# Involution tap matrices: pixel-innermost in whole tiles instead of in groups of three pixels

## The chip, the cores and the metric

One core of one Trainium2 chip runs the whole program. The metric is device time in microseconds (us), the median of 3 runs: 1796.4 us before the change (1794.46 to 1797.01). All data are float32.

## The reference, cut to what matters

Four residual layers act on x of shape (4, 256, 56, 56), each on a group-normed input. Layers 0 and 2 are involutions: from the normed input a 1x1 convolution gives 64 channels, a second one gives, for each of 16 groups and each pixel, 49 tap weights, and each output pixel is the weighted sum of its own 7x7 window. Layer 1 is two 3x3 convolutions, layer 3 a gating; the change does not touch them.

```python
h = jnp.einsum('bchw,oc->bohw', x, reduce_w) + reduce_b[None, :, None, None]
kern = jnp.einsum('bchw,oc->bohw', h, span_w) + span_b[None, :, None, None]
kern = kern.reshape(b, G, 1, K * K, Ho, Wo)            # G = 16, K = 7
out = (kern * patches).sum(axis=3)                     # patches: the 7x7 windows
```

## The kernel before, in words

An image is cut into 19 x 7 = 133 tiles of 3 x 8 = 24 pixels (`NT`, `TP`). The windows of the 24 pixels of a tile lie in one field of 9 x 14 = 126 input positions (`Q`). So the involution of a tile and a group is a matrix product: the 126 positions x 16 channels of the input against a matrix of 126 positions x 24 pixels, in which each pixel has its 49 weights at its own window and zeros elsewhere. These are the tap matrices, the tile `kt`.

Work goes by units: an image b (4) and a half of the channels cb (2), so 8 units in layer 0 and 8 in layer 2. A unit has two stages, one after the other on TensorE.

The first stage, `tap_matrices`, makes `kt` for 8 groups, 24 pixels and 133 tiles, in 32 steps n. A step handles two groups and three pixels (`PB` = 3): TensorE multiplies a weight field by the hidden channels `hp` (line 593, moving operand 133 tiles in one run), six products into one of four pairs of PSUM banks. Then an eviction adds the bias and copies to `kt`. Of three steps in a row, the first two are evicted by VectorE, one instruction for 2 x 3 x 133 = 798 elements a partition (line 611), and the third by ScalarE, six instructions of 133 elements (line 604). So a unit has 22 evictions by VectorE and 10 by ScalarE. `hooks` puts small steps of other work (group-norm sums, loads, channel means) between the steps n. `kt` has one buffer: the next unit's first eviction comes after this unit's last product.

The second stage, `apply`, goes over 7 columns of tiles, tx. For each column and each tile row it multiplies the windows `xw` (stationary) by a slice of `kt` (moving, line 635): 10 tile rows with 4 groups at once (96 moving columns, two products side by side in the array, over 64 output channels each), then 9 tile rows with 2 groups at once (48 moving columns, four side by side). ScalarE takes the first group of the result out of PSUM (line 648 in layer 0, 650 in layer 2), VectorE adds the other groups (655), and GpSimd (660, layer 0) or VectorE (662, layer 2) adds it to the image. After the products of a column, TensorE transposes the strip of a column three ahead (line 406), ScalarE copies it out (418), DMAs on the SP queue and, in layer 0, one on GpSimd's make shifted copies (424, 426), and GpSimd (391, layer 0) or ScalarE (389, layer 2) writes the next strip into the only strip buffer. The next column's transposes wait for that.

The order on each engine is the order in which the program writes the instructions: `in_order` ties each instruction to the one before it on its engine. Nothing is reordered when one takes longer.

In the layout before, `kt` is [126, 8 groups, 8 triples of pixels, 133 tiles, 3 pixels]. An eviction by VectorE writes, for each of two groups, 399 elements in one run. One by ScalarE writes every third element, 12 bytes apart. A slice for line 635 is a group's 24 pixels of one tile: 8 runs of 12 bytes, 1596 bytes apart.

Of the kernel before, what the change touches and what calls it, by code (L numbers as in the profile page):

```python
# [10 lines left out]
F32 = mybir.dt.float32  # L11
# [13 lines left out]
GB = P // GC  # L25
# [10 lines left out]
Q = QY * QX  # L36
NTY, NTX = -(-H // TY), W // TX
NT = NTY * NTX
TP = TY * TX
# [4 lines left out]
PB = 3  # L44
# [27 lines left out]
def net_kernel(  # L72
# [226 lines left out]
    def involution_layer(layer, xin, xout, red, span, sb, xs_of, ahead=None, pending=None):  # L299

        with ExitStack() as es:
            wpool = es.enter_context(tc.tile_pool(name="iw", bufs=1))
            big = es.enter_context(tc.tile_pool(name="ibig", bufs=1))
# [3 lines left out]
            def two_banks():  # L307

                return banks.tile([P, 2, 512], F32, name="ps")
# [83 lines left out]
            def window(ty):  # L393

                k, j = divmod(ty, TY)
                return (0, NSB, 2 * NSB - 1)[j] + k
# [185 lines left out]
            def tap_matrices(b, cb, hooks):  # L582

                hp = h_of[b]
                kt = big.tile([Q, GB, TP // PB, NT, PB], F32, name="kt")
                for n in range(GB // 2 * TP // PB):
                    gp, pb = divmod(n, TP // PB)
                    ps = two_banks()
                    for k in range(PB):
                        py, px = divmod(pb * PB + k, TX)  # L590
                        z0 = ZF - py * QX - px
                        for i in range(2):
                            nc.tensor.matmul(  # L593
                                ps[:Q, i, k * NT : (k + 1) * NT],
                                z_sb[i * R : (i + 1) * R, cb * GB // 2 + gp, z0 : z0 + Q],
                                hp[i * R : (i + 1) * R, py, px].rearrange("p a t -> p (a t)"),
                                start=True,
                                stop=True,
                            )
                    g0, p0 = 2 * gp, pb * PB  # L600
                    if n % 3 == 2:
                        for i in range(2):
                            for k in range(PB):
                                nc.scalar.activation(  # L604
                                    kt[:, g0 + i, pb, :, k],
                                    ps[:Q, i, k * NT : (k + 1) * NT],
                                    AF.Identity,
                                    bias=zb_sb[:, cb * GB + g0 + i, p0 + k : p0 + k + 1],
                                )
                    else:  # L610
                        nc.vector.tensor_tensor(  # L611
                            kt[:, g0 : g0 + 2, pb],
                            ps[:Q, :, : PB * NT].rearrange("q i (k t) -> q i t k", k=PB),
                            zb_sb[:, cb * GB + g0 : cb * GB + g0 + 2, p0 : p0 + PB]
                            .unsqueeze(2)
                            .to_broadcast([Q, 2, NT, PB]),
                            ALU.add,
                        )
                    for h in hooks.get(n, ()):
                        h()  # L620
                return kt

            def apply(b, cb, kt, tx, xw):

                img = xs_of[b, cb].rearrange("p (h w) -> p h w", w=W)
                y0 = 0
                for ng, tys, nty, rows in O_PARTS:
                    pair = two_banks()
                    nb, m = len(tys), ng * GC
                    v = pair[:, :nb, : ng * nty * TP].rearrange("p i (e n) -> p i e n", e=ng)  # L630
                    for i in range(nb):
                        for k in range(nty):
                            ty = tys[i] + k
                            for j in range(P // m):
                                nc.tensor.matmul(  # L635
                                    v[m * j : m * j + m, i, :, k * TP : (k + 1) * TP],
                                    xw[:, window(ty), m * j : m * j + m],
                                    kt[:, ng * j : ng * j + ng, :, ty * NTX + tx, :],
                                    start=True,
                                    stop=True,  # L640
                                )
                    n = rows // nb * TX
                    o = [v[:, :, e, :n] for e in range(ng)]
                    un = work.tile([P, 2, O_PARTS[0][3] // 2 * TX], F32, name="un")
                    un = un.rearrange("p i n -> p (i n)")[:, : rows * TX]
                    part = un.rearrange("p (i n) -> p i n", i=nb)
                    if layer == 0:
                        nc.scalar.mul(part, o[0], bn["par"][ng][:, 0:1])  # L648
                    else:
                        nc.scalar.activation(  # L650
                            part, o[0], AF.Identity, bias=bn["t4"][:, cb : cb + 1], scale=bn["s4"][ng][:, 0, cb : cb + 1]
                        )
                    for e in range(1, ng):
                        s = bn["par"][ng][:, e : e + 1] if layer == 0 else bn["s4"][ng][:, e, cb : cb + 1]
                        nc.vector.scalar_tensor_tensor(part, o[e], s, part, ALU.mult, ALU.add)  # L655
                    dst = img[:, y0 : y0 + rows, tx * TX : (tx + 1) * TX]
                    y0 += rows
                    u = un.rearrange("p (r x) -> p r x", x=TX)
                    if layer == 0:
                        nc.gpsimd.tensor_tensor(dst, u, dst, ALU.add)  # L660
                    else:
                        nc.vector.scalar_tensor_tensor(dst, u, 0.0, dst, ALU.max, ALU.add)
# [355 lines left out]
            for u, (b, cb) in enumerate(units):  # L1018
                hooks = hooks0 if u == 0 else {}
                if prev is not None:  # L1020
                    pb, pc, st, last_sums = prev
# [31 lines left out]
                elif last_image:  # L1053
                    place(hooks, g2, (1,))
                    hooks.setdefault(16, []).append(ahead[0])
                kt = tap_matrices(b, cb, hooks)

                begin_windows()
# [48 lines left out]
                for tx in range(NTX):  # L1107
                    if layer == 2 and u == len(units) - 1 and tx == NTX - 1:
                        column_sums(tx - 1)
                    for f in early[tx]:  # L1110
                        f()
                    apply(b, cb, kt, tx, xws[u * NTX + tx])
                    next_windows()
                    next_strip()
                    if tx > 0 and not (layer == 2 and u == len(units) - 1 and tx == NTX - 1):
                        column_sums(tx - 1)
                    for f in late[tx]:
                        f()
# [640 lines left out]
```

## Time and profile before

| | us |
|---|---|
| median of 3 runs | 1796.4 |
| span of the profiled execution | 1791.4 |
| PE busy in it | 1716.7 (96%) |
| VectorE (DVE) busy | 1385.3 (77%) |
| ScalarE (ACT) busy | 813.5 (45%) |
| GpSimd (POOL) busy | 406.2 (23%) |

The profiled execution's own time is its span from the first to the last instruction; what lies around the span makes up the 5.0 us by which the median of the runs is longer. In the trace each float32 product of the program is two weight loads and two matmuls (PEld and PE), so line 593 has 6144 matmuls for 3072 products. A line of the groups names the source line, the engine, the operation, what is written and read, the shapes, and the count; then busy time, mean duration of one in ns, and the idle time of the engine before it with what ended it. Durations of neighbours on an engine overlap, so the distance from start to start is shorter than the duration. A line of the timeline has the start in us, the time from the first start to the last end, and the same names; x112 at its end means that 112 instructions are merged in it.

### The profile page before, as it was taken

The page shows a single profiled execution, that of the slowest core. Times are in us where ns is not written, and L with a number is a line of the kernel's source. Part 1 is how long each engine was busy: PE and PEld are TensorE (multiplying, and loading weights), DVE is VectorE, ACT ScalarE, POOL GpSimd, SP SyncE. Part 2 cuts the span into 40 slices and gives each one's busy share as a digit, 9 for nine tenths or more (in the row PEclk, how much of TensorE's full clock was granted, in tenths as well). Part 3 has the DMA queues.
Part 4 walks back from the last instruction along what each step waited for, and adds up shares of the span by engine and source line. Part 5 has one row for each costly group of instructions (what it writes and reads, how often), then busy time and mean ns, then how long its engine had stood idle before and what let it go on. Part 6 is the DMA issues. An engine that isn't in the chain of part 4 may idle for free.

```text
span 1791.4 us, 55774 instructions
## 1 busy us (share of the span) xinstructions
PE 1716.7 (96%) x24040; PEld 1507.5 (84%) x24040; DVE 1385.3 (77%) x2745; ACT 813.5 (45%) x1882; POOL 406.2 (23%) x627
## 2 busy tenths in 40 slices
PE   6999999999999999999999999999999999999998
PEld 4998988889978988898889888986888887788886
DVE  2777787767778988988898889885777778687775
ACT  2555556555533222222323132111767667567564
POOL 2224422444320000000000000001000355463572
PEclk9999999999989999999999999999999999999997
DMA  2445444633653021211111111122344567566653
GB/s 86 135 151 170 140 146 134 196 107 119 204 171 105 32 75 51 76 33 64 58 68 44 52 63 37 44 110 73 122 164 156 162 213 220 169 223 189 183 154 115
DMA packets 66003, 215.76 MB, mean 120 GB/s; under 512 B 13237, under 2 KB 20926, under 8 KB 62046
## 3 DMA queue, kind: packets, MB, share of 16 engines
q1 hardware_dynamic: 49262, 145.37, 25.9%
q0 software_dynamic: 14656, 64.77, 11.3%
q8 instruction: 190, 3.11, 0.7%
q10 hardware_dynamic: 1840, 2.05, 0.4%
q14 instruction: 55, 0.45, 0.1%
HBM read 76.30 MB, written 49.15 MB: 70 GB/s over the span
## 4 chain that ended last, share of the span: by engine, by line
PE 68%; DVE 19%; ACT 4%; DMA 4%; issue 3%; POOL 2%; SPq 1%; POOLq 0%; ACTq 0%; DVEq 0%
PE mm L1523 17%; PE ps L593 14%; PE ps L635 14%; PE mm L1441 9%; DVE kt L611 6%; PE mm L1412 5%; PE ps L406 3%; DMA xw<-xw 3%; DVE un L655 3%; PE ps L469 1%; DVE res L1516 1%; DVE xs L1375 1%; DVE st L1105 1%; ACT kt L604 1%; ACT hp L488 1%
## 5 line engine op out<-in xcount | busy, mean ns | idle before, releaser
L635 PE MATMUL ps<-kt,xw 126*32 126x48 f32 (+1 forms) x12544 | 381.8, 235 | 27.8 <-issue 12.2
L635 PEld LDWEIGHTS ps<-kt,xw 126*32 126x32 f32 (+1 forms) x12544 | 341.9, 121 | 74.5 <-issue 45.5
L593 PE MATMUL ps<-hp,z_sb 64*126 64x133 f32 x6144 | 383.2, 279 | 8.4 <-DVE kt L611 4.6
L1523 PE MATMUL mm<-v,u_sb 128*128 128x280 f32 (+1 forms) x1728 | 383.5, 383 | 1.9 <-DVE u_sb L1254 1.5
L593 PEld LDWEIGHTS ps<-hp,z_sb 64*126 64x126 f32 x6144 | 363.6, 185 | 24.4 <-DVE kt L611 6.8
L611 DVE TENSOR_TENSOR kt<-ps,zb_sb 126x798 f32<-126x798 f32 x352 | 332.9, 980 | 60.4 <-PE ps L593 49.2
L1523 PEld LDWEIGHTS mm<-v,u_sb 128*128 128x128 f32 x1728 | 326.1, 189 | 56.3 <-DVE u_sb L1254 1.9
L604 ACT ACTIVATE kt<-ps,zb_sb 126x133 f32<-126x133 f32 x960 | 280.1, 441 | 107.3 <-PE ps L593 107.3
L1441 PE MATMUL mm<-v,u_sb 128*128 128x252 f32 (+1 forms) x936 | 209.5, 384 | 0.0
L1441 PEld LDWEIGHTS mm<-v,u_sb 128*128 128x128 f32 x936 | 176.4, 189 | 30.5 <-issue 0.8
L655 DVE SCALAR_TENSOR_TENSOR un<-ps,s,un 128x240 f32<-128x240 f32 x224 | 102.6, 458 | 86.7 <-ACT un L650 79.9
L1560 POOL DMA_DIRECT2D x<-xs x24 | 13.1, 547 | 680.1 <-DVE xs L1559 426.5
L655 DVE SCALAR_TENSOR_TENSOR un<-ps,par_sb,un 128x240 f32<-128x240 f32 x224 | 98.1, 457 | 86.8 <-ACT un L648 82.3
L1508 ACT ACTIVATE res<-xs,shift,norm_sb 128x1120 f32<-128x1120 f32 (+1 forms) x24 | 30.2, 1258 | 236.3 <-DVE xs L1559 107.3
L418 ACT COPY xw<-ps 126x896 f32<-126x896 f32 x112 | 101.2, 905 | 44.0 <-PE ps L406 38.5
L406 PE MATMUL ps<-ident_sb,strip_sb 128*126 128x128 f32 x784 | 111.9, 283 | 8.4 <-POOL strip_sb L391 5.3
L660 POOL TENSOR_TENSOR xs<-un,xs 128x240 f32<-128x240 f32 x112 | 72.1, 664 | 192.2 <-DVE un L655 192.1
L648 ACT ACTIVATE un<-ps,par_sb 128x240 f32<-128x240 f32 x112 | 50.1, 448 | 122.5 <-PE ps L635 120.6
L650 ACT ACTIVATE un<-ps,bn_t,s 128x240 f32<-128x240 f32 x112 | 60.1, 537 | 94.7 <-PE ps L635 88.7
L406 PEld LDWEIGHTS ps<-ident_sb,strip_sb 128*126 128x126 f32 x784 | 85.1, 142 | 19.5 <-POOL strip_sb L391 8.3
L1412 PE MATMUL mm<-xs,u_sb 128*128 128x126 f32 (+1 forms) x792 | 98.7, 277 | 2.3 <-DVE xs L1375 1.3
L1412 PEld LDWEIGHTS mm<-xs,u_sb 128*128 128x128 f32 x792 | 94.4, 191 | 3.7 <-DVE xs L1428 1.6
(256 smaller groups left out, 1903.1 us busy)
## 6 DMA issues: line engine op xcount, KB each, us to landing
xw<-xw SPq DMA_DIRECT2D x168, 252.0 KB
xw<-xw SPq DMA_DIRECT2D x224, 126.0 KB
xw<-xw POOLq DMA_DIRECT2D x56, 252.0 KB, 4.6
xs<-x SPq DMA_DIRECT2D x24, 560.0 KB
x<-xs POOLq DMA_DIRECT2D x8, 1568.0 KB, 7.5
xs<-x SPq DMA_DIRECT2D x8, 1568.0 KB
xs<-in_x_dram SPq DMA_DIRECT2D x6, 1568.0 KB
x<-xs SPq DMA_DIRECT2D x6, 1568.0 KB
```

Source lines behind the costliest of these rows:

```text
L406: nc.tensor.transpose(ps[:Q, k * P : (k + 1) * P], flat[:, k * Q : (k + 1) * Q], ident_sb)
L418: nc.scalar.copy(xw[:, :NSB, :], ps[:Q, : NSB * P].rearrange("q (n c) -> q n c", n=NSB))
L593: nc.tensor.matmul(ps[:Q, i, k * NT : (k + 1) * NT], z_sb[i * R : (i + 1) * R, cb * GB // 2 + gp, z0 : z0 + Q], hp[i * R : (i + 1) * R, py ...
L604: nc.scalar.activation(kt[:, g0 + i, pb, :, k], ps[:Q, i, k * NT : (k + 1) * NT], AF.Identity, bias=zb_sb[:, cb * GB + g0 + i, p0 + k : p0 ...
L611: nc.vector.tensor_tensor(kt[:, g0 : g0 + 2, pb], ps[:Q, :, : PB * NT].rearrange("q i (k t) -> q i t k", k=PB), zb_sb[:, cb * GB + g0 : cb ...
L635: nc.tensor.matmul(v[m * j : m * j + m, i, :, k * TP : (k + 1) * TP], xw[:, window(ty), m * j : m * j + m], kt[:, ng * j : ng * j + ng, :, ...
L650: nc.scalar.activation(part, o[0], AF.Identity, bias=bn["t4"][:, cb : cb + 1], scale=bn["s4"][ng][:, 0, cb : cb + 1])
L655: nc.vector.scalar_tensor_tensor(part, o[e], s, part, ALU.mult, ALU.add)
L660: nc.gpsimd.tensor_tensor(dst, u, dst, ALU.add)
L1412: nc.tensor.matmul(ps[:, co * m : (co + 1) * m], u[ci][:, co * P : (co + 1) * P], v2[:, e, : n // 2, ci * WT : (ci + 1) * WT], start=(ci = ...
L1441: nc.tensor.matmul(ps, u1_sb[:, ci, dy, k, co * P : (co + 1) * P], v[:, k, dy * NB + ci : (dy + n - 1) * NB + ci + 1 : NB, :], start=(j == 0),
L1523: nc.tensor.matmul(ps, u2_sb[:, ci, dy, k, co * P : (co + 1) * P], v[:, k, dy * NB + ci : (dy + n - 1) * NB + ci + 1 : NB, :], start=(j == 0),
```

## The change

`kt` becomes [126, 8 groups, 133 tiles, 24 pixels]. A slice for line 635 is now one run of 24 elements, 96 bytes, for each group. An eviction by VectorE writes 266 runs of 3 elements (12 bytes), 96 bytes apart. One by ScalarE writes 133 single elements, 96 bytes apart. The numbers of instructions, elements, PSUM buffers and bytes of `kt` are the same, and so is the order of the instructions on every engine.

```diff
-                kt = big.tile([Q, GB, TP // PB, NT, PB], F32, name="kt")
+                kt = big.tile([Q, GB, NT, TP], F32, name="kt")
...
                                 nc.scalar.activation(
-                                    kt[:, g0 + i, pb, :, k],
+                                    kt[:, g0 + i, :, p0 + k],
                                     ps[:Q, i, k * NT : (k + 1) * NT],
...
                         nc.vector.tensor_tensor(
-                            kt[:, g0 : g0 + 2, pb],
+                            kt[:, g0 : g0 + 2, :, p0 : p0 + PB],
                             ps[:Q, :, : PB * NT].rearrange("q i (k t) -> q i t k", k=PB),
...
                                     xw[:, window(ty), m * j : m * j + m],
-                                    kt[:, ng * j : ng * j + ng, :, ty * NTX + tx, :],
+                                    kt[:, ng * j : ng * j + ng, ty * NTX + tx, :],
```

## The prediction

> **What bounds the kernel now.** I read the shares of busy time first, then the costliest groups, then the timeline of one first stage and one steady column. Page and groups:
>
> ```profile
> PE 1716.7 (96%) x24040; PEld 1507.5 (84%) x24040; DVE 1385.3 (77%) x2745; ACT 813.5 (45%) x1882; POOL 406.2 (23%) x627
> ...
> L635 PE MATMUL ps<-kt,xw 126*32 126x48 f32 (+1 forms) x12544 | 381.8, 235 | 27.8 <-issue 12.2
> ...
> L611 DVE TENSOR_TENSOR kt<-ps,zb_sb 126x798 f32<-126x798 f32 x352 | 332.9, 980 | 60.4 <-PE ps L593 49.2
> ...
> L604 ACT ACTIVATE kt<-ps,zb_sb 126x133 f32<-126x133 f32 x960 | 280.1, 441 | 107.3 <-PE ps L593 107.3
> ```
>
> PE is the engine that is never idle. Both evictions wait for PE (49.2 and 107.3 us), and PE hardly waits for them (in the row of L593, 383.2 us busy, 4.6 us for L611). But how much slack they have is a matter of the first stage alone. Its timeline (start, length, count):
>
> ```profile
> 299.77 8.29 PE L593 MATMUL ps<-hp,z_sb 64*126 64x133 f32 x140
> ...
> 300.44 1.75 ACT L604 ACTIVATE kt<-ps,zb_sb 126x133 f32<-126x133 f32 x6 [0.36 <-PE ps L593]
> 301.13 1.89 DVE L611 TENSOR_TENSOR kt<-ps,zb_sb 126x798 f32<-126x798 f32 x2 [0.17 <-PE ps L593]
> 302.50 1.75 ACT L604 ACTIVATE kt<-ps,zb_sb 126x133 f32<-126x133 f32 x6 [0.31 <-PE ps L593]
> ```
>
> Three steps take 2.06 us (300.44 to 302.50): PE needs three times 0.69, ScalarE 1.75 of it, VectorE 1.89. The slack of each is 0.2 to 0.3 us. A steady column of the second stage in layer 0:
>
> ```profile
> 201.53 0.99 PEld L635 LDWEIGHTS ps<-kt,xw 126*32 126x32 f32 x72 [0.16 <-issue]
> 201.70 0.47 ACT L648 ACTIVATE un<-ps,par_sb 128x240 f32<-128x240 f32 x1 [1.27 <-PE ps L635]
> ...
> 202.60 0.98 PE L406 MATMUL ps<-ident_sb,strip_sb 128*126 128x128 f32 x7
> ...
> 203.51 3.27 PE L635 MATMUL ps<-kt,xw 126*64 126x96 f32 x112
> ...
> 205.58 0.90 POOL L391 TENSOR_SCALAR strip_sb<-xs,norm_sb 128x616 f32<-128x616 f32 x1
> ...
> 206.71 0.55 PE L406 MATMUL ps<-ident_sb,strip_sb 128*126 128x128 f32 x3
> ```
>
> The column is 4.11 us (202.60 to 206.71), PE running through; but the strip (L391) is ready at 206.48, only 0.2 us before the transposes (L406) that need it.
>
> [...] The trace before has a row for ScalarE at exactly the new step, the bias table (written 24 words apart), and one for VectorE writing runs of three (14 words apart):
>
> ```profile
> L281 ACT COPY zb_sb<-ps x1: 1103/1103/1103, 44.3 to 44.3; 126x384 f32<-126x384 f32 x1
> ```
>
> ```profile
> L383 DVE MEMSET strip_sb<- x16: 198/198/198, 34.3 to 1683.8; 128x168 f32 x16
> ```
>
> Copies of 252 and 896 contiguous elements take 366 ns (L1424) and 905 ns (L418): 0.84 ns an element and 155 ns fixed. So L281 pays (1103 - 155) / 384 = 2.47 ns an element[...]. L383 writes 56 runs of three in at most 198 ns, 3.5 ns a run with everything in it; L611 takes 831/266 = 3.1 ns for a run at 1.04 ns an element. So a run of three shows no large price at a step of 14 words. No row shows it at 24.
>
> **Part 1, ScalarE's evictions: longer, and on the path.** Today 441 ns. Contiguous, the same form with a bias would take 259 + 133 x 0.84 = 371 (fixed part from L726: 448 elements in 634 ns), so the 12-byte step costs (441 - 259) / 133 = 1.37 ns an element now. At 2.47: 259 + 133 x 2.47 = 587, that is +146 ns. Six of them, 1.75 us today, take 1.75 + 6 x 0.146 = 2.63. In all 960 x 0.146 = +140 us of ScalarE, of which the slack takes a part. Where it ends: there are four PSUM pairs, so the products of step n+6, two steps after the next ScalarE step, wait for the group of step n+2. Two groups then take 2.63 + 0.17 (release) + 3 x 0.69 + 0.30 (PE to ScalarE) = 5.17 us, 2.58 a group instead of 2.06: +0.52. (ScalarE alone, back to back at 0.26 + 0.146 each, would give 2.44.) A stage has 10 groups, 9 intervals; some are already 2.8 us because norm steps stall PE (405.56, 407.62, 410.47, 412.52, 415.32 in one stage), and these I leave. 6 x 0.52 = 3.1, and 0.35 at the end, where steps 30 and 31 wait for ScalarE's last group but one: 3.45 a unit. 16 units: **+55 us**. Queued behind the late evictions on ScalarE are only hooks and the next column's L648 or L650; PE waits for them through PSUM, and that is counted.
>
> **Part 2, VectorE's evictions.** [...] I take 0.10, because L383 speaks for the low side. Cover: VectorE is busy 22.7 us of a 24.8 us stage (403 to 428 us); 22 x 0.10 makes 24.9 in a stage that part 1 has stretched to 28. Only the end and the norm steps behind it feel it: 0.2 a unit, **+3 us**. Without part 1 as cover it would be up to 2.2 x 16 = 35.
>
> **Part 3, the products read 24 in one run: a gain.** Today 40 loads with 96-column products take 1.99 us in the trace (the row of 40 at 199.37, just before those shown): less one load's 0.14, 1.85/19 = 97 ns a pair; the 72 with 48 columns 0.88/17 = 52 ns a set of four. Contiguous operands cost 0.85 ns a column: L1523 383.5 us for 1152 x 280 + 576 x 224 columns; and L718, four side by side over 448 columns, 14 in 1.70 us, about 382 ns a set, the same. So packing in the array costs nothing, and 97 against 82 and 52 against 41 are the runs of three: 0.47 and 0.69 ns a run. With 4 and 2 runs left: 84 and 42.4. Gain per column: 20 x 13 + 18 x 9.6 = 0.43 us of PE; x 112 = 48 us if PE sets every column. It does not:
> - Layer 0: next late is the strip. From L648 (201.70) to the next possible transposes (206.48 + 0.17) are 4.95 us; then 0.91 to the products, and 2.06 (203.51 to 205.83 is 2.32, less 0.26) to the next L648: 7.92 us for two columns, 3.96 against 4.11. So five steady columns gain 0.15, the first two 0.3 together, the last 0.43: 1.5 a unit, 12 in layer 0.
> - Layer 2: the strip is ScalarE's, ready about 1.2 us early, so PE's columns gain all. But PE waits 45.5 us in 152 gaps for no visible cause ("issue") before L635 loads, most of it in some 20 of its 56 columns; there I count 0.1. 36 x 0.43 + 2 = 17.5.
>
> Together **-30 us**.
>
> **Sum.** +55 + 3 - 30 = +28 us on the span of 1791.4. The median of the runs stands 5.0 above that span; the same on top gives 1796.4 + 28 = 1824. Nothing else moves: the order on each engine and all counts are equal.
>
> **Rivals.**
> - VectorE takes ScalarE's place (0.20). [...] For it: [...]L281. Against: L383[...].
> - The read gain wins (0.12), **faster**. PE gains 0.43 in all 112 columns (-48) while the stages lengthen by only 2.2 us each, because ScalarE runs at 2.44 and norm stalls absorb the rest (+35): 1783. It decides if a stage grows by less than 3.0 us. For it: layer 2 and the stalled intervals. Against: L391's 0.2 us of slack.
> - The reading gains nothing (0.12): the 97 ns are not the runs but something in loading 64 or 32 columns. Then +58: 1854. Against: L718's sets of four with 32-column loads.
> - My case, 0.51, own range 1805 to 1845. Other mishaps, slower: 0.05.
>
> **How the numbers follow.** The likeliest is 1824. The range runs from the low edge of my case beyond it to VectorE's rival, 1798 to 1880, leaving out most of the faster case (0.11) and about 0.07 above. A measurement here can tell about 0.2% (3.6 us) from no change. Faster 0.11 (0.10 of its rival, 0.01 of mine), within 0.2% 0.07 (0.05 mine, the rest the rival's), slower 0.82.
>
> **What would show it.** L604 at about 587 ns, with groups of six starting 2.4 to 2.6 us apart in an undisturbed stretch; L611 under 1.1 us; 96-column loads of 40 in about 1.7 us, 72 in about 0.83; first stages 3 to 4 us longer; steady columns of layer 0 near 3.95, of layer 2 near 3.7, with L406 waiting for L391 longer than before (PE 5.3 us). I am wrong if L604 stays under 500 ns, if L611 passes 1.2 us, or if the 40 loads still take 1.9.

## The result, and the profile after

The changed kernel takes 1812.0 us (median of 4 runs, 1804.5 to 1813.5) against 1796.7 us for the kernel before beside it: ratio 1.0077, 95% interval 1.0057 to 1.0097. The profiled execution has a span of 1811.7 us against 1791.4.

The same rows as before the change, from the page of the changed kernel, and the row of the products of the first stage:

```profile
PE 1682.9 (93%) x24040; PEld 1464.2 (81%) x24040; DVE 1410.5 (78%) x2745; ACT 875.2 (48%) x1882; POOL 407.2 (22%) x627
...
L593 PE MATMUL ps<-hp,z_sb 64*126 64x133 f32 x6144 | 397.6, 280 | 24.0 <-ACT kt L604 16.2
L611 DVE TENSOR_TENSOR kt<-ps,zb_sb 126x798 f32<-126x798 f32 x352 | 353.5, 1042 | 75.7 <-PE ps L593 62.9
...
L604 ACT ACTIVATE kt<-ps,zb_sb 126x133 f32<-126x133 f32 x960 | 344.5, 609 | 82.2 <-PE ps L593 82.2
L635 PE MATMUL ps<-kt,xw 126*32 126x48 f32 (+1 forms) x12544 | 331.5, 224 | 49.3 <-issue 27.2
```

PE's busy time fell by 34 us: L635 lost 50.3 (381.8 to 331.5), so the products do read faster, and L593 grew by 14.4 (383.2 to 397.6). But the span grew by 20, so PE was idle about 54 us longer. Its idle time has a new owner in L593, ScalarE's eviction L604 (16.2 us; before, the largest was L611 with 4.6), and a grown one in L635, the gaps without a visible cause ("issue", 27.2 against 12.2).

I cut the span into the 16 first stages (from the first L593 to the first L635) and the 16 second stages (from there to the next first L593; the last of layer 0 has the convolutions of layer 1 in it):

| us | before | after | difference |
|---|---|---|---|
| first stages | 437.7 | 474.0 | +36.3 |
| second stages | 1276.4 | 1258.6 | -17.9 |
| ahead of the first, behind the last | 77.3 | 79.1 | +1.8 |

So both halves of the change are there, with opposite signs, and the loss is twice the gain. How far such sums can be trusted, one execution each: the eight first stages of layer 2 differ by up to 2.5 us between kernels whose evictions are the same, those of layer 0, where nothing else is changed, by 0.4 or less. I therefore read small differences from the stages of layer 0.

The end of a first stage of layer 0, where no norm step comes between, before (ScalarE alone) and after:

```profile
421.56 1.75 ACT L604 ACTIVATE kt<-ps,zb_sb 126x133 f32<-126x133 f32 x6 [0.30 <-PE ps L593]
423.68 1.75 ACT L604 ACTIVATE kt<-ps,zb_sb 126x133 f32<-126x133 f32 x6 [0.36 <-PE ps L593]
425.73 1.75 ACT L604 ACTIVATE kt<-ps,zb_sb 126x133 f32<-126x133 f32 x6 [0.30 <-PE ps L593]
```

```profile
427.10 4.38 PE L593 MATMUL ps<-hp,z_sb 64*126 64x133 f32 x72 [0.28 <-ACT kt L604]
428.10 4.18 DVE L611 TENSOR_TENSOR kt<-ps,zb_sb 126x798 f32<-126x798 f32 x4 [0.71 <-PE ps L593]
429.47 4.29 ACT L604 ACTIVATE kt<-ps,zb_sb 126x133 f32<-126x133 f32 x12 [0.36 <-PE ps L593]
...
431.75 4.38 PE L593 MATMUL ps<-hp,z_sb 64*126 64x133 f32 x72 [0.27 <-ACT kt L604]
...
434.12 4.28 ACT L604 ACTIVATE kt<-ps,zb_sb 126x133 f32<-126x133 f32 x12 [0.36 <-PE ps L593]
```

ScalarE now evicts two groups of six without a pause (x12 in 4.29 us), then waits 0.36 us for PE, and PE waits 0.27 us for ScalarE: a loop through the four PSUM pairs. L593 goes on at 431.75, when the group begun at 429.47 has ended. Six steps start 4.65 us apart (427.10 to 431.75). Before, two groups took 4.17 (421.56 to 425.73), in turn 2.12 and 2.05 us apart. A steady column of layer 0:

```profile
446.39 0.99 PE L406 MATMUL ps<-ident_sb,strip_sb 128*126 128x128 f32 x7 [0.70 <-POOL strip_sb L391]
...
447.31 2.77 PE L635 MATMUL ps<-kt,xw 126*64 126x96 f32 x112
...
449.30 1.00 POOL L391 TENSOR_SCALAR strip_sb<-xs,norm_sb 128x784 f32<-128x784 f32 x1
...
450.35 1.11 PE L406 MATMUL ps<-ident_sb,strip_sb 128*126 128x128 f32 x7 [0.26 <-POOL strip_sb L391]
```

The 112 products take 2.77 us instead of 3.27, and PE then waits for the strip (L391), which it didn't in the column before: 446.39 to 450.35 is 3.96 us, against 4.11.

### The profile page after: what moved, and what is told of

Its sections match the earlier page's. It is cut to its first block, busy times and chain, and to the rows that moved or that the text cites. A ratio compares the mean times of both kernels' runs of the same rounds, so it can differ in the third digit from the quotient of the medians.

```text
span 1811.7 us, 55774 instructions
## 1 busy us (share of the span) xinstructions
PE 1682.9 (93%) x24040; PEld 1464.2 (81%) x24040; DVE 1410.5 (78%) x2745; ACT 875.2 (48%) x1882; POOL 407.2 (22%) x627
## 3 DMA queue, kind: packets, MB, share of 16 engines
q10 hardware_dynamic: 1840, 2.05, 0.4%
## 4 chain that ended last, share of the span: by engine, by line
PE 58%; DVE 16%; ACT 14%; DMA 4%; issue 3%; POOL 3%; SPq 1%; POOLq 0%; ACTq 0%; DVEq 0%
PE mm L1523 18%; ACT kt L604 11%; PE ps L635 10%; PE ps L593 9%; PE mm L1441 9%; PE mm L1412 5%; DMA xw<-xw 3%; DVE kt L611 3%; DVE un L655 3%; PE ps L406 3%; PE ps L469 2%; DVE res L1516 1%; POOL strip_sb L391 1%; SPq L424 1%; POOL xs L660 1%
## 5 line engine op out<-in xcount | busy, mean ns | idle before, releaser
L593 PE MATMUL ps<-hp,z_sb 64*126 64x133 f32 x6144 | 397.6, 280 | 24.0 <-ACT kt L604 16.2
L611 DVE TENSOR_TENSOR kt<-ps,zb_sb 126x798 f32<-126x798 f32 x352 | 353.5, 1042 | 75.7 <-PE ps L593 62.9
L593 PEld LDWEIGHTS ps<-hp,z_sb 64*126 64x126 f32 x6144 | 366.6, 186 | 50.9 <-ACT kt L604 32.0
L604 ACT ACTIVATE kt<-ps,zb_sb 126x133 f32<-126x133 f32 x960 | 344.5, 609 | 82.2 <-PE ps L593 82.2
L635 PE MATMUL ps<-kt,xw 126*32 126x48 f32 (+1 forms) x12544 | 331.5, 224 | 49.3 <-issue 27.2
L635 PEld LDWEIGHTS ps<-kt,xw 126*32 126x32 f32 (+1 forms) x12544 | 296.7, 121 | 92.3 <-issue 64.3
L406 PE MATMUL ps<-ident_sb,strip_sb 128*126 128x128 f32 x784 | 111.5, 283 | 18.0 <-POOL strip_sb L391 12.5
L149 POOL TENSOR_TENSOR norm_sb<-norm_sb,mhalf 128x1 f32<-128x1 f32 x32 | 19.7, 619 | 356.8 <-DVE norm_sb L148 356.8
```

Source lines behind the costliest of these rows:

```text
L406: nc.tensor.transpose(ps[:Q, k * P : (k + 1) * P], flat[:, k * Q : (k + 1) * Q], ident_sb)
L593: nc.tensor.matmul(ps[:Q, i, k * NT : (k + 1) * NT], z_sb[i * R : (i + 1) * R, cb * GB // 2 + gp, z0 : z0 + Q], hp[i * R : (i + 1) * R, py ...
L604: nc.scalar.activation(kt[:, g0 + i, :, p0 + k], ps[:Q, i, k * NT : (k + 1) * NT], AF.Identity, bias=zb_sb[:, cb * GB + g0 + i, p0 + k : p ...
L611: nc.vector.tensor_tensor(kt[:, g0 : g0 + 2, :, p0 : p0 + PB], ps[:Q, :, : PB * NT].rearrange("q i (k t) -> q i t k", k=PB), zb_sb[:, cb * ...
L635: nc.tensor.matmul(v[m * j : m * j + m, i, :, k * TP : (k + 1) * TP], xw[:, window(ty), m * j : m * j + m], kt[:, ng * j : ng * j + ng, ty ...
```

## The experiments

My theory after the result: the first stages grow because ScalarE's instructions to `kt` follow each other more slowly, VectorE's longer evictions are covered, and a large part of what L635 gains is given back to the next late thing. The rivals: VectorE's share of the loss is more than it seems; or the gain in L635 is as small as the second stages show.

**The two halves alone.** In e1 `kt` is written in the old layout and read as if it had the new one; in e2 the reverse. `kn` is the same memory, seen in the new layout.

```diff
+ kn = kt.rearrange("q g a t k -> q g (a t k)").rearrange("q g (t p) -> q g t p", p=TP)
e1:
-     kt[:, ng * j : ng * j + ng, :, ty * NTX + tx, :],
+     kn[:, ng * j : ng * j + ng, ty * NTX + tx, :],
e2:
-     kt[:, g0 + i, pb, :, k],
+     kn[:, g0 + i, :, p0 + k],
...
-     kt[:, g0 : g0 + 2, pb],
+     kn[:, g0 : g0 + 2, :, p0 : p0 + PB],
```

> Evictions write as before (one run by VectorE, 12 bytes apart by ScalarE), the products read 24 elements in one run a group, from a view of the same tile; the pixels so read are not those that were written there, so the values of the convolution are mixed up. My theory (the runs of three slow the products, the gain is caught only in part): 96-column pairs 83 ns and 48-column sets 43 ns apart as in the kernel after, first stages as before (438 us in all), second stages 18 to 30 us shorter, time 1767 to 1779. Rival (the products were slow through something that the write layout changes too[...]): pairs stay at 97 to 100, time about 1797. Rival (every column is set by TensorE): 0.48 x 112 = 54 us less, 1743.

> Evictions write 96 bytes apart as in the kernel after, the products read in runs of three as before; again the pixels are mixed up. My theory (the two effects add): first stages 36 us longer than before, second stages as before, time 1830 to 1836. Rival (the effects do not add, since the longer first stages hide waits of the second): 1815 to 1825.

Reading alone: 1775.6 us against 1796.2 beside it (ratio 0.9881, 0.9855 to 0.9908). Writing alone: 1831.0 us (ratio 1.0194, 1.0167 to 1.0220). That is -20.6 and +34.8, together +14.2; the change measured +15.3. The halves add, so each can be explained by itself. The first stages are 440.3 us in e1 and 473.8 in e2, the second 1254.2 and 1279.4: writing costs in the first stage only, reading gains in the second only. Groups of e1 (the edit moves lines by up to 3, L638 is the old L635), first products, then ScalarE's evictions:

```profile
L638 PE MATMUL ps<-kt,xw 126*32 126x48 f32 (+1 forms) x12544 | 327.2, 225 | 45.4 <-issue 28.2
...
L605 ACT ACTIVATE kt<-ps,zb_sb 126x133 f32<-126x133 f32 x960 | 280.8, 442 | 109.4 <-PE ps L594 109.4
```

The issue gaps (28.2 us, against 12.2 before the change) grow with nothing but a faster read; they aren't an effect of the late first stages.

**ScalarE's or VectorE's writes.** e3 and e4 give the new layout to one engine's blocks only, in one `kt` for all units (`first`: the first unit of each layer keeps the old one).

```diff
e3:
-     kt[:, g0 + i, pb, :, k],
+     kt[:, g0 + i, pb, :, k] if first else kn[:, g0 + i, :, p0 + k],
e4:
-     kt[:, g0 : g0 + 2, pb],
+     kt[:, g0 : g0 + 2, pb] if first else kn[:, g0 : g0 + 2, :, p0 : p0 + PB],
```

> Only ScalarE's evictions write 96 bytes apart (in all units but the first of each layer), VectorE's write one run as before, products read as before; kt is mixed up. My theory (ScalarE's group and the four PSUM pairs set the first stage): most of the cost, 14/16 of about 32, time 1822 to 1828, first stages about 2.0 us longer each. Rival (VectorE's slower evictions set the stage): under 10 us, 1797 to 1806.

> Only VectorE's evictions write in runs of three 96 bytes apart (in all units but the first of each layer), ScalarE's write 12 bytes apart as before, products read as before; kt is mixed up. My theory: half of VectorE's evictions (those whose run of three lies over a 16-byte border) take 0.14 us longer, the others nothing, and the stage hides most: 1798 to 1806. Rival (VectorE sets the stage): 1820 or more.

They took 2040.7 us (ratio 1.1352, 1.1321 to 1.1383) and 1980.0 us (1.1022, 1.0997 to 1.1048), far above the sum of everything. The list of VectorE's waits in e3 says why, and so does ScalarE's in e4:

```profile
DVE kt L617 <- ACT kt L610: 254.7, 124, 2.7
```

```profile
ACT kt L610 <- DVE kt L617: 145.7, 74, 2.6
```

With two layouts in one buffer, a block of one engine lies over bytes of several blocks of the other, so the evictions wait for each other: 254.7 us of a kind of wait that neither kernel has. Both expectations failed, and as a price for one engine both runs are useless: that was a flaw in my edit. One thing can be read from e4: with ScalarE's step as before, L617 (the old L611) took 1085 to 1126 ns (medians) for the blocks of four of the eight triples, the same four as in the changed kernel (below).

**A smaller step for ScalarE alone.** e5 keeps the layout and the reads of the kernel before. Only ScalarE's 133 elements are put down in another order, 84 bytes apart in the block, in seven passes of 19 elements (the columns then take tiles in another order).

```diff
-     kt[:, g0 + i, pb, :, k],
-     ps[:Q, i, k * NT : (k + 1) * NT],
+     kt[:, g0 + i, pb]
+     .rearrange("q t k -> q (t k)")
+     .rearrange("q (r c) -> q c r", c=3 * NTX)[:, k * NTX : (k + 1) * NTX],
+     ps[:Q, i, k * NT : (k + 1) * NT].rearrange("q (c r) -> q c r", c=NTX),
```

> The kernel before, but each of ScalarE's evictions writes its 133 elements 84 bytes apart inside the block of 399 elements that this step owns, so no other eviction touches it; VectorE and the products are as before, the pixels in those blocks are mixed up. My theory (ScalarE alone sets the longer first stage[...]): start to start 300 to 327 ns instead of 254, first stages about 28 to 34 us longer in all, time 1822 to 1832. Rival (VectorE's straddling runs make the stage longer): within 5 us of before. Rival (24 words is a special step, others cost less): start to start 255 to 280, time 1797 to 1808.

1809.3 us against 1795.7 (ratio 1.0075, 1.0051 to 1.0100). The row of ScalarE's evictions, and what PE's loads waited for:

```profile
L604 ACT ACTIVATE kt<-ps,zb_sb 126x133 f32<-126x133 f32 x960 | 310.3, 527 | 92.8 <-PE ps L593 85.0
```

```profile
PEld ps L593 <- ACT kt L604: 16.2, 70, 1.0
```

This wait of the loads was 4.5 us before the change and is 32.0 after. The first stages are 451.5 us, +13.8, and the second 1275.2, close to before. So ScalarE's step alone makes the wait of L593 for L604 and a longer first stage: with 84 bytes, 280 ns from start to start inside a group (254 before), +0.86 us a stage; with 96 bytes, 327 ns and +2.27. It makes up the whole +13.5 us of the run. VectorE had no part in it, its evictions stayed at 981 ns. So a longer step for ScalarE is enough to make a loss of this kind, which e3 was to show and couldn't. The price that I had expected at this step, 300 to 327 ns, was wrong: the run ended just above the range of the second rival.

**VectorE's longer evictions.** In the changed kernel I sorted L611 by the triple pb (medians): 971 to 983 ns for pb 0, 3, 4, 7, as before, but 1092 to 1134 for pb 1, 2, 5, 6. These are the ones whose 12 bytes begin at 8 or 12 modulo 16 in `kt`, so that each run lies over a 16-byte border. e6 leaves the layout and gives ten of these sixteen blocks to ScalarE, six to VectorE; in the changed kernel it is six and ten (not eleven, as I wrote in two expectations).

```diff
+ blocks = [divmod(n, TP // PB) for n in range(GB // 2 * TP // PB)]
+ over = [x for x in blocks if x[1] % 4 in (1, 2)]
+ rest = [x for x in blocks if x not in over[:10]]
  for n in range(GB // 2 * TP // PB):
-     gp, pb = divmod(n, TP // PB)
+     gp, pb = over[n // 3] if n % 3 == 2 else rest[n - n // 3 - (n % 3 == 2)]
```

> The kernel after with the order of the 32 steps permuted, so that ScalarE gets ten blocks whose runs of three lie over a 16-byte border and VectorE has only 6 such evictions in a unit instead of 11; results unchanged. My theory (VectorE is not what sets the stage): within 4 us of the kernel after, 1808 to 1815. Rival (VectorE's 0.14 us land on the path): 5 x 0.14 x 16 = 11 us less, about 1801.

1811.2 us (ratio to the kernel before 1.0087, 1.0065 to 1.0109): not told from the changed kernel's 1.0077. In its groups (L614 is the old L611, L607 the old L604):

```profile
L614 DVE TENSOR_TENSOR kt<-ps,zb_sb 126x798 f32<-126x798 f32 x352 | 345.2, 1016 | 80.2 <-PE ps L596 67.1
L607 ACT ACTIVATE kt<-ps,zb_sb 126x133 f32<-126x133 f32 x960 | 344.2, 611 | 79.8 <-PE ps L596 79.8
```

VectorE is 8.3 us shorter (345.2 against 353.5) and the first stages are 471.1 against 474.0 us. But these 2.9 us lie almost all in layer 2, where e7 and e10, with VectorE's evictions as in the changed kernel, are 2.2 and 2.5 us shorter too; in layer 0 it is 0.2. ScalarE's evictions last as long with ten of those blocks as with six: 611 against 609 ns. So VectorE's extra time is covered, as far as these runs can tell.

**The strip.** In layer 0 the columns wait for GpSimd's strip. e7 lets ScalarE write it there too, as in layer 2.

```diff
-                if layer == 2 and len(strips) > 2:
+                if len(strips) > 2:
```

> The kernel after with the strips of layer 0 written by ScalarE (from the third on, as in layer 2) instead of GpSimd. My theory (in layer 0 the gain of the faster products is lost to the wait of the transposes for the strip): the columns of layer 0 go from about 3.9 to 3.65 us, 8 to 14 us less than the kernel after, 1798 to 1804. Rival (the loss is elsewhere: gaps without a visible cause, or the next wait takes its place): within 3 us of the kernel after, 1809 to 1815.

1810.6 us (ratio 1.0095, 1.0068 to 1.0123), no gain, as the rival had it. What PE waited for in e7, the three longest:

```profile
PE ps L635 <- issue: 27.9, 33, 2.4
PE ps L593 <- ACT kt L604: 16.9, 52, 1.1
PE ps L635 <- DMA xw<-xw: 16.7, 19, 2.3
```

The wait for L391 (12.5 us in the changed kernel) is gone, and undisturbed columns of layer 0 reach 3.62 us. Yet the wait for `xw` grew by 2.3 us (14.4 before this edit), and the second stages are 1254.0 against 1258.6 us, with 3.1 of the 4.6 us in layer 0: so much of 12.5 arrives in the profile, and nothing that the times can tell. The strip is a real wait, but behind it stands the next one.

**A layout between.** e8 keeps half tiles together: two runs of 12 pixels for a product, 48 bytes from element to element for the evictions.

```diff
- kt = big.tile([Q, GB, TP // PB, NT, PB], F32, name="kt")
+ kt = big.tile([Q, GB, 2, NT, TP // 2], F32, name="kt")
...
-     kt[:, g0 + i, pb, :, k],
+     kt[:, g0 + i, p0 // 12, :, p0 % 12 + k],
...
-     kt[:, g0 : g0 + 2, pb],
+     kt[:, g0 : g0 + 2, p0 // 12, :, p0 % 12 : p0 % 12 + PB],
```

> The kernel after with the 24 pixels of a tile in two halves of 12, each half a whole array over the tiles: ScalarE writes 48 bytes apart, VectorE runs of three 48 bytes apart, the products read 12 elements in a run. Results unchanged. My theory ([...]runs of 12 read nearly as well as 24): ScalarE start to start near 327 ns, VectorE the same half of evictions at 1.13 us, pairs 84 to 87 ns, time 1808 to 1818. Rival (96 bytes is a bad step, 48 is not): start to start 255 to 280 ns, first stages 20 to 30 us shorter than after, time 1782 to 1795.

1786.2 us against 1795.7 (ratio 0.9949, 0.9930 to 0.9968): faster than both, as the rival had it. My theory, for ScalarE the same price with 48 bytes as with 96 (327 ns from start to start), failed: it was an estimate of mine, and 254 ns were measured. The two rows of its page:

```profile
L635 PE MATMUL ps<-kt,xw 126*32 126x48 f32 (+1 forms) x12544 | 332.9, 225 | 45.3 <-issue 26.2
...
L604 ACT ACTIVATE kt<-ps,zb_sb 126x133 f32<-126x133 f32 x960 | 289.0, 489 | 105.6 <-PE ps L593 105.6
```

The products read runs of 12 as fast as runs of 24 (332.9 against 331.5 us), and ScalarE's instructions start these 254 ns apart, as before the change, although each lasts 48 ns longer. PE hardly waits for L604 any more (1.0 us, before the change 0.9): the first stages are 444.6 us, +6.9 instead of +36.3. This splits the two edits of the change: its gain needs no 96-byte step. It also parts the two engines, as e3 and e4 should have: VectorE's evictions are as long as in the changed kernel (1043 ns), and without ScalarE's late groups the first stages lose 6.9 us.

Four kernels together show what sets the stage. In the stages of layer 0 with the fewest norm steps, ScalarE's group of six lasts 1.75 us before the change, 1.81 in e8, 1.94 in e5 and 2.23 after it; the stage lasts 24.76, 25.21, 25.66 and 27.13. So the stage grows by 0.45, 0.90 and 2.37 us. In e5 and after the change that is some five times what the group grows by, one for every two groups and one at the end; in e8 it is somewhat more, and there VectorE has a part (e11).

**The gaps of layer 2.** L635's issue gaps, those of matmuls and those of loads added up (some of them are the same gap, seen twice), are 57.7 us before the change (12.2 and 45.5) and 91.5 after (27.2 and 64.3). In layer 2 the gating of layer 3 runs beside the columns, with loads and stores. e9 and e10 are the kernels before and after without it.

```diff
-     chunks.extend(gate_chunk(pb, j, c) for j in range(NCHUNK) for c in range(NB))
...
-     late[0] += [lambda b=b, j=j: load_sf(b - 1, j) for j in range(2)]
+     pass
```

> The kernel before, with the gate work that runs beside layer 2 left out (the chunks of the gating and the loads that belong to them, so the last layer's output of the first three images is not written). The partner of the next run. Both theories expect it well below 1796 us, I guess 1740 to 1790, since the unexplained gaps before L635's loads in layer 2 (29.5 us on the weight loads, 9.7 on the matmuls) shrink to under 15 us together if the gate's transfers make them, and stay near 39 us if they don't.

> The changed kernel with the same gate work left out. Theory A: the 0.48 us that a column of layer 2 gains in its products is lost in gaps that the gate's work makes beside it. Without that work the eight second stages of layer 2 gain some 3 us each (24 us instead of about 10), so this kernel differs from the run before it by 0 to +5 us in place of +15. Rival B: the gaps belong to TensorE's own stream of instructions and come wherever products go faster: the difference stays +12 to +18 us, and gaps before L635 in layer 2 stay near 60 us.

1772.1 us (5 runs, 1766.9 to 1774.7) and 1784.3 us (7 runs, 1779.3 to 1786.9): a difference of 12.2, where theory A wanted 0 to 5 and rival B 12 to 18. From the spread of the runs I estimate its error as 4 us, so it can't be told from the 15.3 with the gating. By the time, rival B holds. The gaps before L635, first e9's, then e10's:

```profile
PE ps L635 <- issue: 6.1, 10, 1.5
...
PEld ps L635 <- issue: 33.9, 139, 1.6
```

```profile
PE ps L635 <- issue: 11.9, 20, 1.7
...
PEld ps L635 <- issue: 38.9, 111, 1.9
```

By the gaps, neither holds: 40.0 and 50.8 us, so without the gating they grow by 10.8 us with the faster read, with it by 33.8. In layer 2 alone e9 brings them from 39.2 to 15.8, and e10's are 23.4 us, not the 60 that B wanted. The eight second stages of layer 2 gain 15.5 us here (248.4 to 232.9) and 9.6 with the gating (270.2 to 260.6). The 9.6 is uncertain: with the gating, the kernels that read in runs of three took 265.4 to 270.2 us there (e3 and e4 left out), those that read in longer runs 259.1 to 263.6. So the gating seems to take part of the gain, though the times don't show it; A had the place of most gaps right and their weight wrong.

**Both mends.** e11 is e8 with the dealing out of e6.

> The layout with half tiles (two runs of 12 pixels), with the blocks dealt out so that ScalarE gets ten of the sixteen whose runs of three lie over a 16-byte border, and VectorE six in place of about eleven. If VectorE's longer writes are on the path in this layout, where ScalarE is no longer late, the first stages fall from 444.6 by 2 to 5 us, and the time to 1781 to 1785 us. If the stage is TensorE's there, both stay: 444 and 1786 us.

1784.5 us against 1796.0 (ratio 0.9944, 0.9925 to 0.9963), first stages 442.0 us, -2.6. Most of that is in layer 2 again, but here the undisturbed stages of layer 0 moved too, from 25.21 to 25.10 (in e6 by 0.04 or less). So VectorE's writes are on the path in this layout, but 40% of their extra time is worth only about 0.1 us a stage, less than the 2 to 5 us in all that I had expected. 1.7 us of time can't be told from e8.

## Why the prediction was right, and where its terms were off

The forecast was slower, with the loss in the first stage and a smaller gain in the second: 1824 us, range 1798 to 1880. It is 1812. The mechanism and the signs hold; three sizes were off. Part 1 made the forecast some 19 us too high, part 3 some 12 too low, so the sum came closer than its terms; that was luck.

- **Part 1, +55: measured +36, and the term that failed is the 2.63 us of a group.** The duration was foreseen (587; it is 609). But I added its growth, +146 ns, to the distance between instructions. Measured from start to start, this is 254 ns before and 327 after, +73, while the duration grew by 168: the rest lies over the next instruction. With 327 a group is 5 x 0.327 + 0.609 = 2.24 us, and my loop gives 2.24 + 0.17 + 2.07 + 0.30 = 4.78, close to the 4.65 of the timeline. The same loop with the 1.75 us of before gives 4.29, where 4.17 was measured, and I took 2.06, the shorter of two distances that take turns (2.05 and 2.12), for both; I should have taken the difference of two such sums, not set one against a measured time. Together: 0.52 a group was 0.24. In the traces neighbours overlap by 441 - 254 = 187 ns before and 609 - 327 = 282 after.
- **Part 1, the norm steps that I left out.** I gave them no growth (6 intervals of 9). They grew as well: in the stage at 403 us (411.8 after) such an interval went from 2.80 or 2.85 to 3.28, and the one behind it stayed at 2.05, so that two groups grew as much as two undisturbed ones. Four such growths of 0.47 and 0.48 at the stage's end, where I gave 0.35, make up its +2.37. The trace has the norm step L228 waiting 3.9 us for L604 on PE, with nothing like it before. A stall of PE ahead of the loop was no slack for ScalarE. So this error made the forecast too low, the one above made it too high.
- **Part 2, +3: small, as forecast.** The mean is +0.062 us (980 to 1042 ns) instead of 0.10, which was an estimate. The cover holds: e6 takes away some 40% of the extra time, and the stages of layer 0 are 0.2 us shorter in all, so no more than a fraction of the 3 us shows. The extra time isn't the same for all: the four triples over a 16-byte border take 1092 to 1134 ns, +0.11 to 0.15 us for 266 runs, the others 971 to 983, as before.
- **Part 3, -30: -18 in the profile, -21 in e1.** The gain of a column was well sized: its products take 2.57 us instead of 3.05 from first to last start, 0.48 against my 0.43; times 112, 54 us. What I let through was too much. Layer 0 was to gain 12 and gained 8; layer 2 was to gain 17.5 and gained 10. The limit of layer 0 is the one named: the strip, steady columns of 3.81 to 4.02 where I gave 3.96. But in the first columns and in the units in which other work runs beside, the gain went into gaps and waits, and e7 shows that removing the strip's wait opens others. In layer 2 undisturbed columns take 3.62 us without the gating (e10), and the shortest with it 3.70, but I counted the gaps of 45.5 us as fixed; they grew with every faster read (54.2 to 64.4 with the gating), and the waits of one kind gave way to those of another.
- **The rivals.** VectorE takes over: no, L611 stayed at 1042 ns on average; the 1880 at the top of the range, set for this rival, was an estimate that no run shows. Reading gains nothing: no. The read gain wins: its own condition, a stage that grows by less than 3.0 us, came true (2.27), and the kernel was slower all the same, since its other half, 48 us landing in all columns, failed. It even had the size of the stage (2.2 us), though not through norm stalls that absorb the rest. A condition on one term was no test of a sum of two.
- **The sum.** +36.3 - 17.9 + 1.8 = +20.2 on the span, 20.3 with nothing rounded. Between the medians it is 15.3: before the change the median stands 5.0 us above the span of the profiled execution, after it 0.3. The 5.0 is not all work around the span, as I had it: the executions whose time and span are both on record stand 1.7 to 3.4 us above their own span, all but one by at most 2.3. So the one profiled before was some 3 us faster than its median, and the one after (1813.5 us) 1.5 slower.

What stays open: what the issue gaps are. The profile names no releaser for them. They grow with the speed of the products (40.0 to 50.8 us without the gating, 57.7 to 91.5 with it) and with the gating beside them, whose loads, stores and work on GpSimd no run takes away one by one; and no run tells TensorE's own stream of instructions from a wait that the trace doesn't record.

## What to carry to other kernels

When an operand is laid out anew, price the writer by the distance from start to start of its instructions, and by the duration of the last one alone, and check whether the step in bytes has a bad value; here ScalarE's instructions followed each other as fast with 48 bytes as with 12 (254 ns), but not with 96 (327), and the reader was as well served by runs of 48 bytes as of 96 (83 ns a pair). A saving in a stage with several nearly late partners can shrink to the slack of the next one, as e7's did (4.6 of 12.5 us): count those partners before counting instructions. And a layout between two extremes, which takes the read's gain without the write's price, is worth a run before either extreme is judged.

## What the runs showed of the hardware that I had not expected

- ScalarE, 133 float32 elements from PSUM to `kt`, start to start inside a group: 254 ns with 12 bytes from element to element, 254 with 48, 280 with 84 (in passes of 19 elements), 327 with 96. So of these four steps 12 and 48 bytes have the same price, 84 and 96 a higher one. With 96 it is 2.46 ns an element, as much as L281's 2.47 before the change. L281 writes inside 1.5 KB a partition, an eviction of the changed kernel across 12.8 KB, so a long stretch isn't needed for this price. I have no measured reason.
- With 96 bytes, an eviction by ScalarE lasts 609 ns, and the next one starts after 327. In the stage shown, the last of the group begun at 429.47 runs from 431.09 to 431.70, and L593, which waits for its PSUM pair, goes on 0.05 us behind its end (431.75), not at the start of the next eviction (431.53).
- VectorE's runs of three words at a step of 96 bytes cost nothing (971 to 983 ns an eviction, 980 in one run before the change) unless they lie over a 16-byte border (1092 to 1134).
- TensorE reads a moving operand in runs of 12 words as fast as in runs of 24: 83 ns a pair and 43 ns a set of four both ways, against 100 and 52 with runs of three.
